# Mirroring a quarter of each symmetric product by VectorE and HBM instead of TensorE, in a four-layer graph network

## The chip, the cores and the metric

The kernel runs on one core of a Trainium2 chip. The metric is device time in microseconds, medians of several runs. A ratio is the mean time of one kernel's runs over that of the other kernel's runs of the same rounds, so it is not quite the ratio of the medians that are quoted.

The engines are TensorE (PE; its weight loads are listed as PEld), VectorE (DVE), ScalarE (ACT), GpSimd (POOL) and SyncE (SP). A name with a q, such as ACTq or SPq, is the sequencer of that engine, which takes instructions in program order and also issues transfers.

## The reference, cut to what matters

There are 16 batches of a graph with 1024 nodes and 128 features, in fp32, and four layers. Two of the layers contain a product whose result is a symmetric matrix. Layer 0 has it three times, layer 3 once (there the kernel multiplies gT by hT in one symmetric product, so that the sum with the transpose needs no pass of its own):

```python
# layer 0, three times
h = h @ W + b
nh = h / jnp.maximum(norm, EPS)
cos = jnp.einsum('bij,bkj->bik', nh, nh)      # symmetric, 1024 x 1024
h = jnp.einsum('bpq,bqc->bpc', edge_weight * cos, h)
# layer 3
h = jnp.einsum('bnf,of->bno', x, W_w) + W_b
e = jnp.einsum('bil,bkl->bik', h @ A, h)
e = e + jnp.swapaxes(e, 1, 2)                 # symmetric, 1024 x 1024
att = jax.nn.softmax(jnp.where(adj > 0, e, 0), axis=1) * adj
...
```

Layer 1 multiplies by the adjacency; layer 2 is an attention with tanh and exp. They matter here only as work beside the products.

## The kernel before

Each symmetric product is 8 x 8 blocks of 128 x 128. The kernel multiplies only the blocks on and above the diagonal. It keeps those above the diagonal in SBUF (the tile `above`, copied out of PSUM by ScalarE) and fills the blocks below by transposing the kept ones on TensorE:

```python
def row_of_square(k, j, s, leftT, rightT, above):      # row j of blocks, half s of it
    lo, hi = HALVES[s]
    dst = ps(f"sq_{k}_{j}_{s}")                         # a PSUM bank
    first = max(lo, j)
    if first < hi:
        pe((hi - first) * MM, ..., lambda: nc.tensor.matmul(dst..., cols(leftT.t, j), span(rightT.t, first, hi)))
    n = min(hi, j) - lo
    if n > 0:
        ...                                             # at: the places of the kept blocks
        def mirrored():
            for r, p in enumerate(at):
                nc.tensor.transpose(cols(dst.t, r), cols(above.t, p), ident)
        pe(n * TR, ...)
    return dst
```

The instructions are not written in the order in which they run. Each is recorded as an `Op` with its engine, an assumed duration and what it reads and writes. A planner then orders all of them, up to three batches interleaved, with constants: a period, latencies, and a table `LEADS` with a number for each kind of instruction. What it decides is fixed; every engine then works through its list in order. A transfer is recorded on an engine "DMA" that holds nobody else.

```python
op("DMA", 2.0, [z], [],
   lambda: nc.scalar.dma_start(out[b]..., by_block(z.t)))   # the store of a batch's result
```

## Time and profile before

| | before |
|---|---|
| median of 4 runs | 2550.4 us |
| TensorE busy | 2500 us, 98% |
| VectorE busy | 2004 us, 79% |
| ScalarE busy | 1385 us, 54% |
| DMA queue of SyncE | 143 MB, 30% of 16 engines |
| period of a batch in the middle | 155.3 us |

The period is read from the chain of work that ended last: the same piece, 22 matmuls of 9.44 us, stands there at 882.60 and at 1037.86 us. An engine's row that says how much it was busy does not yet say what it costs: pipelined matmuls overlap, so work on TensorE is priced by the distance between starts. The prediction does that, and shows the lines.

### The profile page before, as it was taken

Reading aid. Unit: us, or ns where it says so; the run is one execution under the profiler, and the core shown is the slowest. Engines: PE = TensorE matmul, PEld = TensorE weight load, DVE = VectorE, ACT = ScalarE, POOL = GpSimd, SP = SyncE. Lnnn points to the kernel's source line nnn. Section 1 sums busy time; section 2 is a strip of 40 time slices with the busy share of each in tenths; the row PEclk is TensorE's granted clock in tenths of the full one; section 3 lists DMA queues with packets and bytes.
Section 4 is the critical chain, followed back from the end, with each engine's and each line's share of the span. In section 5 each row is a group of like instructions: output and inputs, shape, how many; then the busy total and the mean of one; then the engine's idle time right before and its main releaser. Section 6 shows DMA issues by size and latency. Waiting matters only on the chain.

```text
span 2548.1 us, 35510 instructions
## 1 busy us (share of the span) xinstructions
PE 2500.2 (98%) x12714; PEld 1674.1 (66%) x12714; DVE 2003.7 (79%) x5070; ACT 1384.7 (54%) x2609; POOL 215.3 (8%) x134
## 2 busy tenths in 40 slices
PE   7999999999999999999999999999999999999996
PEld 4567576775667666676666767657676666765763
DVE  6658979787787968879687796877878778796777
ACT  4426575644646556455654656447464564554365
POOL 1001000101101010010100101010010100100000
PEclk9999999999999999999999999999999999999998
DMA  9320706133070430604216052340614306042100
GB/s 138 68 67 4 146 1 101 49 52 98 1 124 26 59 91 11 133 7 67 83 26 123 1 84 66 46 104 1 116 34 59 91 8 122 21 59 75 30 12 17
DMA packets 588641, 154.32 MB, mean 61 GB/s; under 512 B 537520, under 2 KB 572080, under 8 KB 588464
## 3 DMA queue, kind: packets, MB, share of 16 engines
q1 hardware_dynamic: 567552, 142.65, 29.6%
q10 hardware_dynamic: 20912, 9.40, 1.4%
q8 instruction: 100, 1.64, 0.3%
q14 instruction: 77, 0.63, 0.1%
HBM read 143.61 MB, written 8.39 MB: 60 GB/s over the span
## 4 chain that ended last, share of the span: by engine, by line
PE 91%; DVE 4%; ACT 2%; DMA 1%; SPq 1%; issue 1%; POOLq 0%; POOL 0%; ACTq 0%; DVEq 0%
PE acc L620 33%; PE acc L631 18%; PE sq L587 17%; PE sq L597 7%; PE psP L453 5%; PE py L463 2%; PE py L792 2%; PE ps_hTn L443 1%; PE ph L463 1%; PE ps_hnT L443 1%; PE pg L463 1%; PE psN L453 1%; SPq L673 1%; DVE e L921 1%; DVE top L930 1%; ACT e L934 1%
## 5 line engine op out<-in xcount | busy, mean ns | idle before, releaser
L740 DVE SCALAR_TENSOR_TENSOR ew<-sq,rn,adjT 128x512 f32<-128x512 f32 x768 | 555.0, 741 | 133.9 <-PE sq L597 84.4
L609 ACT COPY above<-sq 128x512 f32<-128x512 f32 (+3 forms) x640 | 285.2, 455 | 491.6 <-DVE ew L740 431.1
L620 PE MATMUL acc<-ew,h 128*128 128x512 f32 x1024 | 498.4, 597 | 1.6 <-DVE ew L740 1.5
L587 PE MATMUL sq<-hTn 128*128 128x512 f32 (+3 forms) x1152 | 452.2, 489 | 2.4 <-ACT hTn L475 2.4
L597 PEld LDWEIGHTS sq<-ident,above 128*128 128x128 f32 x1792 | 226.5, 141 | 156.9 <-issue 108.3
L597 PE MATMUL sq<-ident,above 128*128 128x128 f32 x1792 | 299.8, 273 | 4.9 <-ACT above L609 4.9
L620 PEld LDWEIGHTS acc<-ew,h 128*128 128x128 f32 x1024 | 177.2, 191 | 147.0 <-issue 100.2
L587 PEld LDWEIGHTS sq<-hTn 128*128 128x128 f32 x1152 | 189.3, 191 | 121.2 <-issue 84.6
L631 PEld LDWEIGHTS acc<-h,ew 128*128 128x128 f32 x2048 | 244.1, 192 | 31.7 <-issue 14.4
L631 PEld LDWEIGHTS acc<-h,e 128*128 128x128 f32 x2048 | 239.9, 193 | 30.3 <-issue 27.1
L631 PE MATMUL acc<-h,ew 128*128 128x128 f32 x2048 | 251.5, 275 | 0.3 <-DVE ew L740 0.3
L631 PE MATMUL acc<-h,e 128*128 128x129 f32 x2048 | 241.1, 276 | 2.5 <-DVE e L862 2.5
L934 ACT ACTIVATE e<-e,top 128x1024 f32<-128x1024 f32 x128 | 146.9, 1148 | 171.9 <-DVE top L930 166.5
L620 PE MATMUL acc<-e,hs 128*128 128x512 f32 x512 | 235.7, 596 | 1.5 <-DVE e L941 1.5
L620 PE MATMUL acc<-adjL,hn 128*128 128x512 f32 x512 | 236.8, 593 | 0.3 <-ACT hn L567 0.2
L862 DVE SCALAR_TENSOR_TENSOR e<-adjT,e 128x512 f32<-128x512 f32 x256 | 165.2, 686 | 64.0 <-ACT e L858 63.8
L436 POOL TENSOR_TENSOR rstd<-ve,mhalf 128x8 f32<-128x8 f32 x64 | 104.8, 1637 | 1096.0 <-DVE ve L528 1092.6
L684 ACT ACTIVATE adjT<-adjT 128x1024 f32<-128x1024 f32 x128 | 135.3, 1057 | 95.5 <-DVE adjT L681 78.5
L921 DVE SCALAR_TENSOR_TENSOR e<-adjT,sq 128x512 f32<-128x512 f32 x256 | 170.5, 675 | 6.5 <-PE sq L587 6.5
L941 DVE TENSOR_TENSOR e<-e,adjT 128x512 f32<-128x512 f32 x256 | 167.3, 679 | 0.0
L681 DVE STREAM_TRANSPOSE adjT<-adjT 128x1024 f32<-128x1024 f32 x128 | 155.8, 1229 | 8.8 <-DMA adjT<-in_adj_dram 4.6
L620 PEld LDWEIGHTS acc<-adjL,hn 128*128 128x128 f32 x512 | 93.8, 190 | 101.4 <-issue 88.6
(121 smaller groups left out, 3260.8 us busy)
## 6 DMA issues: line engine op xcount, KB each, us to landing
adjT<-in_adj_dram SPq DMA_DIRECT2D x512, 128.0 KB, 3.9
adjL<-in_adj_dram SPq DMA_DIRECT2D x128, 512.0 KB, 4.0
x<-in_x_dram SPq DMA_DIRECT2D x16, 512.0 KB, 5.1
out_dram<-z ACTq DMA_DIRECT2D x16, 512.0 KB, 5.6
b<-in_L_gnn_b_dram ACTq DMA_DIRECT2D x4, 64.0 KB, 4.5
w<-in_L_gnn_W_dram ACTq DMA_DIRECT2D x2, 128.0 KB, 3.9
w<-in_L_gnn_W_dram ACTq DMA_DIRECT2D x3, 64.0 KB, 3.5
w2e<-in_L_gnn_W_dram ACTq DMA_DIRECT2D x1, 64.0 KB, 2.7
```

What stands on the lines that cost most here:

```text
L453: nc.tensor.matmul(dst.t[:, (c - lo) * n : (c - lo + 1) * n], cols(srcT.t, c), w, start=True, stop=True)
L587: lambda: nc.tensor.matmul(dst.t[:, (first - lo) * P :], cols(leftT.t, j), span(rightT.t, first, hi), start=True, stop=True),
L597: nc.tensor.transpose(cols(dst.t, r), cols(above.t, p), ident)
L609: lambda: nc.scalar.copy(span(above.t, p, p + hi - first), dst.t[:, (first - lo) * P :]),
L620: lambda s=s, lo=lo, hi=hi: nc.tensor.matmul(acc[s].t, cols(h.t, at, w), span(ew.t, lo, hi), start=(j == 0), stop=(j == NB - 1)),
L631: nc.tensor.matmul(a.t[:, (c - lo) * n : (c - lo + 1) * n], cols(ew.t, c), h.t[:, j * w : j * w + n], start=(j == 0 and c == lo), stop=(j ...
L681: dve(V(N), [t], [t], lambda t=t: nc.vector.transpose(t.t, t.t), True)
L740: lambda pc=pc, ew=ew, rn=rn, j=j, lo=lo, hi=hi: nc.vector.scalar_tensor_tensor(span(ew.t, lo, hi), pc.t, rn.t[:, j : j + 1], span(aT[j].t ...
L862: lambda e=e, j=j, lo=lo, hi=hi: nc.vector.scalar_tensor_tensor(span(e.t, lo, hi), span(aT[j].t, lo, hi), 0.0, span(e.t, lo, hi), op0=ALU. ...
L921: lambda e=e, p=p, j=j, lo=lo, hi=hi: nc.vector.scalar_tensor_tensor(span(e.t, lo, hi), span(aT[j].t, lo, hi), 0.0, p.t, op0=ALU.is_gt, op ...
L934: lambda e=e, top=top, tot=tot: nc.scalar.activation(e.t[:, 0:N], e.t[:, 0:N], AF.Exp, bias=top.t, accum_out=tot.t),
L941: lambda e=e, j=j, lo=lo, hi=hi: nc.vector.tensor_mul(span(e.t, lo, hi), span(e.t, lo, hi), span(aT[j].t, lo, hi)),
```

## The change

The lower left quarter of each product (rows 4 to 7, columns 0 to 3) is the mirror of the upper right one. The change takes its 16 transposes from TensorE. VectorE turns each 32 x 32 square of the upper right quarter while it reads it out of PSUM. In each product two stores to HBM and eight reads, ten transfers, then put the squares in their places in a tile `got`. The masking passes read `got` from SBUF. This is done in batches 1 to 13. In layer 3, h^T is now a transpose of h rather than a second product. And the buffers and the planner's constants are new.

```diff
+    FAR = range(1, B - 2)
...
+            if self.by_dma and j >= QUARTER and s == 0:
+                q = j - QUARTER
+                return self.got, lambda: self.got.t.rearrange("p (r c d) -> p c r d", r=QUARTER, d=P)[:, q]
...
+            if self.by_dma and j < QUARTER and s == 1:
+                p, above = PLACE[j, lo], self.above
+                dve(
+                    V(HALF), [read], [blk(above, p, p + 4)],
+                    lambda: nc.vector.transpose(span(above.t, p, p + 4), read.t),
+                )
+                if j % 2:
+                    self.send(j - 1, j + 1)
+                return
...
+        def send(self, lo, hi):
+            ...                                  # store of two rows of four blocks, 512 KB
+            op("DMA", 0.35 * (hi - lo), [blk(above, at, end)], [by_hbm], ..., lat=2.2)
+            def squares_to_places():
+                src = by_hbm.t.rearrange("(x j) (g i) -> g j x i", j=SQ, i=SQ)
+                for g in range(P // SQ):
+                    dst = span(got.t, lo * 4, hi * 4)[g * SQ : (g + 1) * SQ]
+                    ...
+                    nc.sync.dma_start(dst.rearrange("p (x i) -> p x i", i=SQ), src[g])
+            op("DMA", 1.8 * (hi - lo), [by_hbm], [blk(got, lo * 4, hi * 4)], squares_to_places, lat=2.4)
...
-        hT, gT = w4(f"h3T_{b}"), w4(f"gT_{b}")
-            for dst, w, v, name in ((hT, w3e[:, 0:D], wb3col, "ph"), (gT, wg, bg, "pg")):
...
+        hT = flipped(h, f"h3T_{b}", w=E3)
...
-    PERIOD, LAST, AHEAD, WINDOW = 74.0, 9.0, 2, 0.02
+    PERIOD, LAST, AHEAD, WINDOW = 66.0, 23.0, 2, 0.05
...                                              # POOLS, KINDS and all of LEADS replaced
```

## The prediction

> **What bounds the kernel now.** I read the page of the profiled execution first, its busy table and the chain of work that ended last:
>
> ```profile
> PE 2500.2 (98%) x12714; PEld 1674.1 (66%) x12714; DVE 2003.7 (79%) x5070; ACT 1384.7 (54%) x2609; POOL 215.3 (8%) x134
> PE 91%; DVE 4%; ACT 2%; DMA 1%; SPq 1%; issue 1%; POOLq 0%; POOL 0%; ACTq 0%; DVEq 0%
> ```
>
> TensorE is busy 98% of the span and carries 91% of the last chain; VectorE is the next, at 79%. Busy time of pipelined matmuls can mislead, so I asked for the busy time by stretch. Two runs of 22 back-to-back L620 matmuls lie 155.2 us apart again and again in the chain, so that is the period of one of the 16 batches. One period, then the first 100 us and the last 99 us (engines PE, PEld, DVE, ACT, POOL, then clock, DMA share, GB/s):
>
> ```profile
> 1041.00:1196.20 155.20, 155.03 (x795) 104.21 (x794) 124.77 (x317) 86.17 (x163) 13.35 (x8) 1.00 0.31 62
> ...
> 0.00:100.00 100.00, 80.92 (x327) 48.05 (x328) 70.45 (x170) 47.95 (x95) 12.20 (x13) 0.97 0.91 131
> ...
> 2450.00:2549.00 99.00, 73.99 (x356) 48.34 (x355) 80.97 (x187) 61.44 (x110) 6.40 (x3) 0.91 0.04 11
> ```
>
> In the middle TensorE lacks 0.17 us of work in a period, VectorE has 30 us free, the DMA engines are busy 31%. About 19 us are lost at the start and 25 at the end. A microsecond taken from TensorE in the middle is therefore a microsecond off the span, as long as VectorE and the transfers keep up.
>
> To price TensorE's work I need the distance between instructions, not their mean duration, which holds the pipeline's depth. The order in time and the chain give it:
>
> ```profile
> 1008.35 1.04 PE L597 MATMUL sq<-ident,above 128*128 128x128 f32 x8
> ...
> 1037.86 9.44 PE acc L620 x22
> ```
>
> Eight transposes take 1.04 us, one alone lasts 0.273 us, so the next starts (1.04 - 0.273)/7 = 0.110 us later. A 512-wide matmul instruction takes 9.44/22 = 0.429 us; a program's 512-wide fp32 product is two of these, 0.858 us. Sixteen 128-wide instructions in 1.95 us give 0.112 us each in the same way. Priced so, all of TensorE's work sums to about 2477 us, which agrees with the busy time.
>
> **What the Trainium skill says.** "Perfetto Trace Analysis", section "Identifying the Most-Contended Engine", says that matmul occupancy does not tell the distance from roofline. This trace agrees that occupancy isn't peak rate (weight loads are busy 66%), but the bound is real: the chain runs through TensorE and its gaps are 0.1%. The gain has to come from fewer instructions.
>
> "VectorE: DVE Perf Modes", section "The three transpose paths", says VectorE's transpose turns 32x32 blocks only, and warns against a plain copy whose strides do the transposing. That is why the change needs a second leg: the blocks are turned on VectorE, and the way through HBM moves whole 32-element rows of squares to their places. The kernel before does the same for the adjacency, and its trace shows both legs: the square transpose of 128x1024 takes 1229 ns, and the transfers are priced below.
>
> "DMA: Bandwidth & Descriptors", sections "Specifications" and "Anatomy of one DMA", says that runs below 512 B miss line rate, and that the fixed cost, some 2 us, is mostly the receipt of the last byte, heaviest into HBM. The trace agrees: a 128 KB transfer in 128-byte runs lands after 2.2 us at best, 3.9 in the median; 512 KB to HBM in 512-byte runs (the store of the output, the very shape of the new store) after 3.2 us at best, 5.6 in the median.
>
> **The change, part by part.** It acts in 13 of the 16 batches (1 to 13), in 4 products each, so 52 squares.
>
> *Removed from TensorE.* In a square, rows 4 to 7 no longer mirror their left half: 4 x 4 = 16 of the 28 transposes go. 16 x 52 = 832 of 1792, and 832 x 0.110 = 91.5 us. The rows they come from and where they go:
>
> ```profile
> L597 PE MATMUL sq<-ident,above 128*128 128x128 f32 x1792 | 299.8, 273 | 4.9 <-ACT above L609 4.9
> L463 PE MATMUL ph<-hnT,w3e 128*128 128x512 f32 x64 | 30.3, 594 | 0.2 <-ACT hnT L475 0.2
> L941 DVE TENSOR_TENSOR e<-e,adjT 128x512 f32<-128x512 f32 x256 | 167.3, 679 | 0.0
> ```
>
> The second row is layer 3's separate projection for h^T: 64 instructions x 0.429 = 27.5 us. It becomes 8 transposes in a batch, 128 x 0.110 = 14.1 us. Saved: 13.4 us, in all 16 batches. TensorE loses 91.5 + 13.4 = 105 us in all: 7.0 + 0.8 = 7.9 us in a period, from 155.2 to 147.3.
>
> *Added to VectorE.* Four transposes of 128x512 from PSUM in each square, 208 in all. I take the occupied time of another pass of that size, 167.3/256 = 0.65 us (third row above): 136 us, 10.5 us in a period. The masking passes that now read the returned blocks from SBUF instead of PSUM keep their count and, as passes with both inputs in SBUF take 679 to 686 ns and those with one in PSUM 675, their price. VectorE goes from 124.8 to 135.3 us of a 147.3 us period, 92%, and from 2004 to 2140 us in all. It stays below TensorE, but its free time shrinks from 30 to 12 us a period.
>
> *Removed from ScalarE.* The 208 512-wide copies of those half rows, about 0.5 us each: 100 us. It is at 54% and off the path, so this is worth nothing by itself.
>
> *Added to the transfers.* In each square two stores of 512 KB and eight reads of 128 KB in 128-byte runs, 4 + 4 MB in a period beside the adjacency. Rates, from two stretches of the kernel before, the first with adjacency squares, the second with 4 KB rows:
>
> ```profile
> 1012.00:1017.00 5.00, 5.00 (x29) 3.41 (x28) 5.00 (x9) 2.34 (x5) 0.00 (x0) 1.00 0.73 108
> ...
> 1067.00:1072.00 5.00, 5.00 (x19) 2.74 (x18) 0.85 (x3) 0.60 (x2) 1.90 (x1) 1.00 0.73 231
> ```
>
> 108/0.73 = 148 GB/s for the small runs when the engines are full, about 316 for the large. 4.2 MB of small runs take 28 us, 4.2 MB of stores some 13 to 20 us. The DMA share goes from 48 us of 155 to about 92 of 147, 60 to 65%: not a bound in the mean.
>
> *The latency of one mirroring.* Store 3.2 to 5.6 us; four reads, 512 KB at 148 GB/s = 3.5 us, plus a landing tail of about 2 us: 9 to 11 us from the last transpose to the data. In the built order of VectorE's instructions, what stands between the last transpose of a square and its first use of the returned blocks is, in one product of layer 0, twelve 512-wide passes (12 x 0.65), eight statistics (8 x 0.21), eight aggregations (8 x 0.08) and a small one: 10.3 us. By the same counting two further products of a period have about 10 us and layer 3's about 20. So the latency is just hidden where the DMA engines are free, and short by a few microseconds where adjacency loads stand in the way.
>
> *The new plan order and buffers.* The built order is again periodic from batch 3 on, with TensorE's priced work in a period at 146.8 us. At both ends it is like the old one: about 40 us of TensorE work stand behind the last layer-3 projection, formerly and now. I book nothing for the ends.
>
> **Sum.** 2551.7 - 105 = 2447 us if TensorE stays as full as it is. I add 13 us: about 1 us a period of TensorE waiting, because VectorE at 92% with transfer waits of a few microseconds in its in-order stream cannot follow as loosely as at 80%. That gives 2460 us, 3.6% faster. The 1 us is my choice; nothing of before measures it.
>
> **Rivals.** *The way through HBM is late.* If each of the three tight products of a period waits 5 us, VectorE has 135 + 15 = 150 us, above TensorE's 147: period about 151, some 50 us of the gain lost, 2500 us. For it: the store of that shape took 5.4 to 5.9 us in the middle of the run, and the queue issues in order, so a read waiting for its store holds up loads behind it. Against: VectorE has 12 us of slack and the reads' rate fits.
>
> *VectorE becomes the local bound.* In the stretch of the old kernel from 1012 to 1042 us it was busy 5.00 of every 5 us, and TensorE still had work queued. Ten more microseconds of it, most in such stretches, and PSUM banks that now wait for two VectorE readers, could cost 2 to 4 us a period: 2475 to 2500 us. Against: during layer 1 VectorE was idle over 80% for ten microseconds, so a new order has something to fill.
>
> *The saving lies beside something else.* If transposes hid in the weight loads or in waits, removing them would give little, and the time would stay near 2540. Against: their spacing, 0.110 us, is in the priced sum that fits the span, and no gaps remain for them to hide in.
>
> *The new order is better at the ends.* 44 us are lost there; 10 us regained makes 2440.
>
> **Range and chances.** Most of what can go wrong costs 15 to 50 us, and only the ends can bring more than 105. 80% range: 2436 to 2502. Faster by over 2% means below 2500.7, that is, losing less than half of the saving: 0.87. Within 2%: 0.10. Slower by over 2% would need transfer waits of some 12 us a period beyond the saving: 0.03.
>
> **What will show it.** Right: TensorE's mirrored transposes at 960 with a period near 148 us and TensorE above 99% in it; 208 VectorE transposes near 0.68 us; VectorE near 87% of the span; waits of VectorE for the returned blocks under 100 us in all, and hardly any of them reaching TensorE. Wrong: TensorE idle for VectorE's products by several microseconds a period (the second rival), or those preceded by VectorE waiting for a transfer (the first), or a period below 147.

## The result, and the profile after

The changed kernel takes 2484.18 us (2483.74 to 2484.56, 4 runs) against 2550.43 us (2548.58 to 2552.96, 4 runs). The ratio is 0.974, with a 95% interval of 0.9723 to 0.9756. It is faster by 2.6%. The time is inside the predicted range, but of the 105 us that were to be saved, 66 arrived.

The busy table and the chain that ended last, of the changed kernel:

```profile
PE 2410.6 (97%) x11946; PEld 1588.7 (64%) x11946; DVE 2119.4 (85%) x5278; ACT 1287.1 (52%) x2401; POOL 214.4 (9%) x134
PE 78%; DVE 9%; ACT 7%; issue 2%; DMA 1%; SPq 1%; ACTq 0%; POOL 0%; POOLq 0%; DVEq 0%
```

TensorE carries 78% of the chain instead of 91%. The rest has gone to VectorE and ScalarE, so TensorE now waits for something. One period, and the two ends (engines in the order PE, PEld, DVE, ACT, POOL, then clock, DMA share, GB/s):

```profile
868.44:1018.40 149.96, 148.17 (x736) 97.54 (x735) 133.53 (x333) 78.79 (x147) 13.09 (x8) 1.00 0.58 119
...
0.00:100.00 100.00, 77.42 (x300) 44.69 (x301) 70.07 (x165) 45.04 (x89) 12.20 (x13) 0.95 0.89 158
2383.00:2482.00 99.00, 74.75 (x358) 48.63 (x356) 82.59 (x191) 61.46 (x109) 5.43 (x3) 0.88 0.04 11
```

The period is 150.0 us; the prediction's price of TensorE's work made 147.3. TensorE is idle 1.8 us of it; the other 0.9 us are counted as busy. The ends lose as much as before, within 4 us. So what is missing is missing in the middle, 13 times 2.7 us or about 35.

The parts of the change, in the table of groups and in the table of issues (for a transfer, the last number is the median time to landing in us):

```profile
L619 PE MATMUL sq<-ident,above 128*128 128x128 f32 x960 | 174.4, 275 | 27.8 <-ACT above L641 27.8
L631 DVE STREAM_TRANSPOSE above<-sq 128x512 f32<-128x512 f32 x208 | 147.0, 707 | 10.5 <-PE sq L609 9.1
L791 DVE SCALAR_TENSOR_TENSOR ew<-got,rn,adjT 128x512 f32<-128x512 f32 x156 | 112.8, 743 | 1.8
...
by_hbm<-above SPq DMA_DIRECT2D x104, 512.0 KB, 3.2
got<-by_hbm SPq DMA_DIRECT2D x416, 128.0 KB, 3.0
```

The counts are as predicted, 960 and 208. A transpose of VectorE takes 707 ns where near 680 was forecast; its start-to-start distance from the next pass is 0.62 us (in the chain below). The passes that read `got` stood idle 1.8 us in all, and no transfer is named for it; the 52 passes of layer 3 that read it (L973) stood idle 0.0 us. So VectorE never waits for the returned blocks. What grew is the first row's wait: TensorE stood idle 27.8 us for `above`, ScalarE's copy, where it was 4.9.

Where that comes from is shown by the chain in order of time (start, length, what) in the same period:

```profile
927.75 1.52 PE sq L609 x4
...
930.70 0.62 DVE above L631
931.32 2.07 DVE z L505 x8
...
936.33 0.96 ACT e L910
937.29 2.60 issue
939.90 0.38 ACTq L1056
...
949.43 0.02 issue
949.45 0.06 DVE e L914
...
954.39 2.09 DVE ew L791 x3
956.48 0.02 issue
956.50 0.49 ACT above L641
956.99 0.04 issue
957.03 0.33 PE sq L619
```

From the end back: TensorE at 957.03 waited for ScalarE's copy of a row of layer 0. That copy waited for VectorE's masking pass of the same row. VectorE came late to it because it had been following ScalarE through the tanh/exp tiles of layer 2 (L914 after L910), one by one. And ScalarE was late with those because between 937.29 and 939.90 it did nothing, and then issued L1056. L1056 is the store of the previous batch's result. ScalarE's own line of time around it:

```profile
936.24 1.06 ACT L910 ACTIVATE e<-e 128x1024 f32<-128x1024 f32 x1
939.90 0.38 ACTq L1056 DMA_DIRECT2D out_dram<-z  x1
940.32 2.19 ACT L906 ACTIVATE e<-s,h 128x1024 f32<-128x1024 f32 x2 [3.03 <-issue]
```

ScalarE idles 3.03 us before a tanh (L906) whose inputs had long been there. The profile calls it "issue" because the tanh itself waits for nothing; it is the store before it in the queue that waits for z, which VectorE finishes at 939.8. How long the store's wait stood in ScalarE's queue, in ns as minimum, median and maximum, for the kernel before and the changed one:

```profile
L1002 ACTq EVENT_SEMAPHORE  x16: 17/982/3401, 305.2 to 2540.4; - x16
```

```profile
L1056 ACTq EVENT_SEMAPHORE  x15: 17/4820/4825, 334.9 to 2474.1; - x15
```

The median went from 1.0 to 4.8 us. The wait is in the kernel before as well, but there, in the period that I looked at, the next thing in ScalarE's queue was a pass of layer 1 that waited for TensorE anyway. In the list of waits (us in total, times, longest) the changed kernel has

```profile
ACT e L906 <- issue: 36.6, 13, 3.1
```

or 2.8 us each, about one in every period; the kernel before has no such entry.

This is theory A: the new order puts the store in front of urgent ScalarE work, because the planner thinks that a store holds nobody. Theory B: VectorE, at 89% of a period, is simply too full, and the store is only where it shows. Theory C: the transfers are late or in the way. Theory D: the new plan order costs something by itself.

### The profile page after: what moved, and what is told of

The parts are those of the page before. It is cut to its first block, busy times and chain, and to the rows that moved or that the text cites. A ratio compares the mean times of both kernels' runs of the same rounds, so it can differ in the third digit from the quotient of the medians. Undisturbed runs are those within 1.5% of the kernel's fastest.

```text
span 2481.8 us, 34726 instructions
## 1 busy us (share of the span) xinstructions
PE 2410.6 (97%) x11946; PEld 1588.7 (64%) x11946; DVE 2119.4 (85%) x5278; ACT 1287.1 (52%) x2401; POOL 214.4 (9%) x134
## 4 chain that ended last, share of the span: by engine, by line
PE 78%; DVE 9%; ACT 7%; issue 2%; DMA 1%; SPq 1%; ACTq 0%; POOL 0%; POOLq 0%; DVEq 0%
PE acc L671 31%; PE sq L609 17%; PE acc L682 11%; PE psP L461 6%; PE sq L619 4%; ACT e L906 3%; DVE ew L791 3%; ACT e L910 3%; PE py L844 2%; PE py L471 2%; DVE e L914 2%; PE ps_hTn L451 1%; DVE z L505 1%; PE pg L471 1%; PE ps_hnT L451 1%
## 5 line engine op out<-in xcount | busy, mean ns | idle before, releaser
L791 DVE SCALAR_TENSOR_TENSOR ew<-sq,rn,adjT 128x512 f32<-128x512 f32 x612 | 436.9, 739 | 68.2 <-PE sq L619 32.0
L671 PE MATMUL acc<-ew,h 128*128 128x512 f32 x1024 | 480.6, 597 | 4.7 <-DVE ew L791 4.5
L609 PE MATMUL sq<-hTn 128*128 128x512 f32 (+3 forms) x1152 | 441.3, 489 | 0.4 <-ACT hTn L483 0.4
L641 ACT COPY above<-sq 128x384 f32<-128x384 f32 (+3 forms) x432 | 169.2, 394 | 403.9 <-DVE ew L791 366.5
L682 PE MATMUL acc<-h,e 128*128 128x129 f32 x2048 | 249.5, 277 | 2.8 <-DVE e L914 1.5
L619 PEld LDWEIGHTS sq<-ident,above 128*128 128x128 f32 x960 | 125.7, 141 | 142.2 <-issue 74.0
L619 PE MATMUL sq<-ident,above 128*128 128x128 f32 x960 | 174.4, 275 | 27.8 <-ACT above L641 27.8
L914 DVE SCALAR_TENSOR_TENSOR e<-adjT,e 128x512 f32<-128x512 f32 x256 | 162.0, 683 | 41.9 <-ACT e L910 41.9
L732 DVE STREAM_TRANSPOSE adjT<-adjT 128x1024 f32<-128x1024 f32 x128 | 155.2, 1225 | 17.8 <-DMA adjT<-in_adj_dram 10.9
L906 ACT ACTIVATE e<-s,h 128x1024 f32<-128x1024 f32 x128 | 143.1, 1141 | 38.4 <-issue 36.6
L631 DVE STREAM_TRANSPOSE above<-sq 128x512 f32<-128x512 f32 x208 | 147.0, 707 | 10.5 <-PE sq L609 9.1
```

The costliest lines, as they stand in the source:

```text
L609: lambda: nc.tensor.matmul(dst.t[:, (first - lo) * P :], cols(leftT.t, j), span(rightT.t, first, hi), start=True, stop=True),
L641: lambda: nc.scalar.copy(span(above.t, p, p + hi - first), read.t[:, (first - lo) * P :]),
L671: lambda s=s, lo=lo, hi=hi: nc.tensor.matmul(acc[s].t, cols(h.t, at, w), span(ew.t, lo, hi), start=(j == 0), stop=(j == NB - 1)),
L682: nc.tensor.matmul(a.t[:, (c - lo) * n : (c - lo + 1) * n], cols(ew.t, c), h.t[:, j * w : j * w + n], start=(j == 0 and c == lo), stop=(j ...
L732: dve(V(N), [t], [t], lambda t=t: nc.vector.transpose(t.t, t.t), True)
L791: lambda view=view, ew=ew, rn=rn, j=j, lo=lo, hi=hi: nc.vector.scalar_tensor_tensor(by_block(span(ew.t, lo, hi), D, 4), view(), rn.t[:, j ...
```

## The experiments

### The store on SyncE's queue

```diff
-            lambda: nc.scalar.dma_start(out[b]..., by_block(z.t)),
+            lambda: nc.sync.dma_start(out[b]..., by_block(z.t)),
```

> The changed kernel with one word altered: the store of the output is issued from SyncE's queue instead of ScalarE's. Every instruction of TensorE, VectorE and GpSimd stands in the same order. Theory A (ScalarE stands behind its own store: its queue waits 4.8 us in the median for z, then the tanh/exp pairs of layer 2 start 2.8 us late, VectorE follows them, and TensorE waits some 2 us for a copy of layer 0): the period falls from 150.0 to about 148 us, TensorE's waits for the copy above (27.8 us) go to under 5, the time to about 2458 us, 1.0% below the changed kernel. Theory B (VectorE at 89% of the period is what TensorE waits for) and theory C (the transfers, which share SyncE's queue, are late): no change at 2484, or with C a few us slower.

Measured: 2453.79 us (2453.39 to 2454.57, 4 runs; before 2551.11), ratio 0.9617, interval 0.9604 to 0.963. That is 30.4 us below the changed kernel, 4 us more than theory A asked for. One forecast of theory A was missed: TensorE's wait for ScalarE's copy fell from 27.8 us, but to 9.0 and not under 5. That wait, one period, and ScalarE's line of time at the same place:

```profile
PE sq L619 <- ACT above L641: 9.0, 5, 2.3
```

```profile
788.72:936.07 147.35, 147.35 (x737) 97.54 (x736) 133.70 (x333) 78.55 (x148) 13.35 (x8) 1.00 0.60 122
```

```profile
929.50 1.06 ACT L910 ACTIVATE e<-e 128x1024 f32<-128x1024 f32 x1
930.46 2.18 ACT L906 ACTIVATE e<-s,h 128x1024 f32<-128x1024 f32 x2
```

The tanh pair now follows the exp with no gap. TensorE is busy 147.35 us of 147.35, and the period is the one that the prediction priced. Since TensorE, VectorE and GpSimd have the very same lists here, theory A holds for 30 of the missing 35 us, and B, C and D don't explain those 30. This version beats both kernels.

### The same word in the kernel before

The edit is the same, in the kernel before.

> Control: the kernel before with the same word altered. There ScalarE's queue waits only 1.0 us in the median at the store and TensorE never waits in the middle, so theory A expects 2550 us as before, within 3 us. If moving the store helps every kernel (a cheaper queue, say), this one would gain 20 us too, and theory A falls.

Measured: 2551.60 us (13 runs) against 2551.11, ratio 1.000, interval 0.9992 to 1.0009. The queue by itself is worth nothing. It is the wait in front of urgent work that costs.

### The plan told of the hold

```diff
-        op(
-            "DMA", 2.0, [z], [],
+        o = op(
+            "ACT", 0.4, [z], [],
             lambda: nc.scalar.dma_start(out[b]..., by_block(z.t)),
         )
+        o.key = "3 DMA z"
```

> The changed kernel with the store still in ScalarE's queue, but the plan told so: it is booked as a ScalarE instruction that waits for z, not as a transfer that holds nobody. The order of all engines changes with it. Theory A (the plan did not know that the store holds ScalarE): the plan keeps other ScalarE work ahead of the store, the hold per batch falls from 2.8 us to under 1, and the time is within 12 us of the 2454 of the kernel with the store on SyncE. If it is the ScalarE queue as such that is slow at stores, it stays near 2484.

Measured: 2621.58 us (4 runs), ratio 1.0284, so worse than both theories said. Theory A's forecast, within 12 us of 2454, was not met. The hold did become rarer: "ACT e L906 <- issue" is down to 18.5 us in 6 occurrences, though the store's wait is still 3.4 us in the median. But the whole order changed with it, and in the new order TensorE is busy only 289 of 300 us in the middle. So the run neither supports nor refutes theory A: what the changed order cost and what the rarer hold gained can't be told apart. It does show that this planner's order can go bad when one cost is altered under a table of leads that was made for another.

### No mirroring, new plan

```diff
-    FAR = range(1, B - 2)
+    FAR = ()
```

> The changed kernel with no batch mirrored by VectorE and HBM: only layer 3's h^T turned from h, and the new plan constants, remain. TensorE's priced work falls by 13.4 us against before, to 2463. If the plan itself is sound: 2538 us, 0.5% faster than before. The plan's constants were sought for the other set of instructions, so theory D (the new plan order costs something by itself) expects 2550 or more.

Measured: 2580.78 us (4 runs), ratio 1.0115, interval 1.0101 to 1.0129. Theory D is right for this set of instructions: with 13 us less work for TensorE than the kernel before, it is 30 us slower. Here the store's wait is 17 ns in the median, so it isn't the store. The period is 156.35 us. The plan's constants are not better or worse as such; they fit the set with mirroring.

### The old constants with mirroring

```diff
-    PERIOD, LAST, AHEAD, WINDOW = 66.0, 23.0, 2, 0.05
+    PERIOD, LAST, AHEAD, WINDOW = 74.0, 9.0, 2, 0.02
     LEADS = {
-        ...                      # all values of the changed kernel
+        ...                      # all values of the kernel before
```

with the store on SyncE.

> Store on SyncE, mirroring and buffers as in the changed kernel, but the plan's constants (PERIOD, LAST, WINDOW, LEADS) of the kernel before. The instructions are the same, in another order. If the order must be sought for the very set of instructions, as the run without mirroring suggests (30 us slower than before in the new order): 2490 to 2600. If any order of this planner would do: about 2455.

Measured: 2712.43 us (4 runs), ratio 1.0627: outside my range, 259 us worse than the same instructions in the new order. TensorE carries only 56% of its chain. So the new order is no ornament of the change: in the old order, mirroring by VectorE would have lost. The old table has no entries for the new instructions, which then count as 0; how much of the 259 us that makes, I did not test.

### All batches mirrored

```diff
-    FAR = range(1, B - 2)
+    FAR = range(B)
```

with the store on SyncE.

> Store on SyncE and all 16 batches mirrored by VectorE and HBM instead of 13: TensorE's priced work falls by another 3 x 7.0 = 21 us, which would make 2433 if the ends can follow and the order in the middle stays as good. But the plan's order changes everywhere, and VectorE has under 1 us of slack a period: I expect 2440 to 2520, so rather a loss than a gain.

Measured: 2729.21 us (4 runs), ratio 1.0693, again far outside my range. The extra mirroring is worth 21 us of TensorE at most; the order, which changed everywhere with it, cost more than ten times that. In the middle, where the instructions are the same, TensorE is busy 280 of 300 us. Whether mirroring at the ends is good or bad can't be read from this run.

### TensorE's remaining transposes twice

```diff
                         nc.tensor.transpose(cols(dst.t, r), cols(above.t, p), ident)
+                        nc.tensor.transpose(cols(dst.t, r), cols(above.t, p), ident)
```

with the store on SyncE.

> Store on SyncE, same order, and each of TensorE's remaining 960 mirrored transposes done twice. If a transpose of TensorE costs its spacing, one for one, as the prediction priced it: 960 x 0.110 = 105 us more, 2559 us (VectorE then has slack again, so nothing else is added). If transposes partly lie beside other work, it is clearly less, say under 2520.

Measured: 2544.87 us (2542.81 to 2546.31, 7 runs), ratio 0.9974, interval 0.9964 to 0.9985. It costs 91 us, between the two forecasts (105 us, or under 66), and so is far from hidden. In the middle the period goes from 147.35 to 152.17 us, 4.8 for 48 transposes priced at 0.110, or 5.3. The missing 0.5 us are short delays that the busy table does not show and that are gone with the doubled work: before doubling, three runs of matmuls of the period took longer in the chain than the same matmuls elsewhere (16 in 2.02 us instead of 1.79, 12 in 5.29 instead of 5.15, 6 in 2.64 instead of 2.58), 0.43 us in all, and with doubling none does. In the run itself the doubled transposes follow each other at 0.11 us. The rest of the difference to 105 us must lie outside the middle, where TensorE waits anyway; I did not follow it. So the price that the prediction put on a transpose is right where TensorE is full.

### VectorE's transposes twice

```diff
-                    lambda: nc.vector.transpose(span(above.t, p, p + 4), read.t),
+                    twice,      # the same transpose, two times
```

(The edit is shortened: `twice` calls the transpose two times.) First with the store on ScalarE as in the changed kernel:

> The changed kernel with each of the 208 square transposes of VectorE done twice, in the same order: VectorE gains 208 x 0.62 = 129 us of work, 9.9 us a period, which makes 133.6 + 9.9 = 143.5 us of a 150.0 us period. Theory B: VectorE's load is what costs, so nearly all of it comes out: the period grows by 5 to 10 us, the time to 2550 to 2610. Theory A: VectorE has slack except behind the late tanh/exp pairs, and the period grows by under 4 us, to under 2535.

Measured: 2588.42 us (4 runs), ratio 1.0144; 104 us more than the changed kernel, of 129 us of added work. This is what theory B forecast, and theory A's forecast (under 2535) failed: VectorE has no 9.9 us a period to spare. Then with the store on SyncE:

> Store on SyncE, all 208 square transposes done twice: 129 us more VectorE work, 9.9 us a period, VectorE at 143.9 of 147.3 us if nothing waits. With the store on ScalarE the same doubling cost 104 us. If the 104 us were VectorE's order alone, it costs 95 to 110 us here too (2550 to 2565); if part of it was the two waits meeting (the hold of ScalarE grew from 2.8 to 3.9 us in that run), it costs 60 to 90 us (2514 to 2544).

Measured: 2564.20 us (2558.73 to 2569.84, 4 runs), ratio 1.0053; 110 us more than without doubling. So the cost is there without the hold of ScalarE, and that the hold grew in the other run added nothing. Then with only row 0's transpose doubled, 52 of 208:

> Store on SyncE, and one of the four square transposes of each square (row 0's) done twice: 52 x 0.62 = 32 us more VectorE work, 2.5 us a period, VectorE at 134.0 + 2.5 = 136.5 of 147.3 us. If VectorE has slack now (TensorE's gaps are nil in the middle): under 5 us more, below 2459. If it is the bound beside TensorE (theory B): about 30 us more, 2484.

Measured: 2474.26 us (2472.69 to 2476.19, 4 runs), ratio 0.970; 20.5 us more for 32 us of work. Neither forecast was met; the truth lies between. The three runs together: the first 32 us of added work cost 20.5, the next 97 cost 90. VectorE shows 13.6 us of idle time in a period of 147.35 us, yet of 2.5 us put in, only about 1 disappeared in it: the same piece of the chain stands at 1538.35 and 1687.30 us, a period of 148.95 us. The trace of the version without doubling shows where the idle time lies. In ten-microsecond stretches of one period VectorE is busy 9.99 and 10.00 us from 976 to 996 us, where transposes of its squares stand, and only 5.43 from 1036 to 1046. Part of the cost may also come by another way, as a later transpose makes its transfers later: in the run with row 0 doubled the chain of one period holds the landing of a read, 2.85 us. I did not separate the two. Theory B is therefore not the cause of the 30 us that came back with the store moved, but VectorE has about 1 us a period left before it costs.

### The reads twice

```diff
                         nc.sync.dma_start(dst.rearrange("p (x i) -> p x i", i=SQ), src[g])
+                        nc.sync.dma_start(dst.rearrange("p (x i) -> p x i", i=SQ), src[g])
```

with the store on SyncE.

> Store on SyncE, and every read of the mirrored blocks back from HBM done twice (16 reads of 128 KB in a square instead of 8): the DMA engines' share rises from 59% to about 80% of the middle, and each square's data comes some 4 us later, as the second read of a place must be waited for too. If the transfers have that much slack, the time stays within 5 us of 2454; theory C (they arrive just in time) expects 3 waits of 3 to 4 us a period in VectorE and 30 to 100 us more.

Measured: 3402.43 us (4 runs), ratio 1.3339. This was a badly made experiment: the second read writes where the first one writes, so SyncE waits for the first to land before it issues the second, as the list of SyncE's waits says (total us, times, longest):

```profile
SPq L663 <- DMA got<-by_hbm: 958.5, 416, 5.0
```

416 waits of 2.3 us turn the reads, which otherwise run beside each other, into a row. It measures that and not the load. So I mended it, with the second reads going to a tile of their own:

```diff
+                        spare = span(scratch, 0, (hi - lo) * 4)[g * SQ : (g + 1) * SQ]
+                        nc.sync.dma_start(spare.rearrange("p (x i) -> p x i", i=SQ), src[g])
```

> Store on SyncE, same order, and behind each read of mirrored blocks a second read of the same data into a tile that nobody uses, so that no read waits for its twin (that wait spoilt the earlier doubling of the reads). SyncE issues 8 more transfers in a square at some 0.6 us each and the DMA share goes to about 80%; the last wanted read is issued some 2 us later. If the transfers have slack: within 10 us of 2454. If they arrive just in time (theory C): 3 late squares a period at 2 us or more, which with VectorE at its limit comes out in full: 2500 to 2530.

Measured: 2718.80 us (4 runs), ratio 1.0653; 265 us more, beyond theory C's range. The first use of returned blocks in a square, in VectorE's line of time and in the list of waits:

```profile
1045.65 1.41 DVE L794 SCALAR_TENSOR_TENSOR ew<-got,rn,adjT 128x512 f32<-128x512 f32 x2 [3.55 <-DMA got<-by_hbm]
...
DVE ew L794 <- DMA got<-by_hbm: 111.2, 31, 6.0
DVE e L976 <- DMA got<-by_hbm: 57.1, 12, 5.8
```

Now VectorE does wait for the transfers, 168 us in 43 waits. Two things can have delayed the last wanted read, and the run does not separate them. Eight more transfers of a square are issued in SyncE's queue, at 0.56 us and more each. And although the DMA share is 63% over the span, an average misleads here: from 1030 to 1045 us, where the reads for the first line above stand, it is 1.03 (the view's figure can pass 1), and from 1080 to 1165 us 0.98, so the engines are about full when the squares move; without the spare reads it is 0.92 from 985 to 1050 us. The wanted reads land after 3.8 us in the median instead of 3.1. The slack of the good version can be read from its own trace. In one period the last read of a layer-0 square is issued at about 940.3 us and lands about 2.9 us later, at 943.2; VectorE uses it at 944.65. Followed in the same way, with the median landing of their group of reads, two other squares of the period had about 1.5 and 2 us. So the transfers of the version with the store on SyncE are on time by one to two microseconds, as estimated from one period and from landings that are partly medians. Theory C is not the cause of the missing time, but there is little room before it would cost; the forecast that the transfers have slack (within 10 us of 2454) failed. Why 168 us of direct waits become 265 us of time I did not follow further; waits for adjacency loads also grew, to 52.0 us from 15.5.

## Why the prediction was right or wrong

**What bounds the kernel, and the removed work: right.** The step "105 us in all: 7.0 + 0.8 = 7.9 us in a period, from 155.2 to 147.3" is confirmed by the run with the store on SyncE: 147.35 us, TensorE busy all of it by the table, 2453.8 us against the 2447 of the sum. (The period of the kernel before is 155.26 us by the chain; the prediction read 155.2.) The doubled transposes confirm the price from the other side. The rival that the saving lies beside something else is refuted.

**VectorE: right in size, too comfortable in words.** It was priced at 2140 us in all and 135.3 us a period; it measured 2119 and 133.5 to 133.7. "Its free time shrinks from 30 to 12 us a period" is right as idle time (13.6 in the good version), but it is not slack: the doubling of a few transposes found about 1 us. The rival "VectorE becomes the local bound" did not take the missing time, since moving the store gave 30 us back with VectorE's work unchanged; but its reason, stretches in which VectorE has no gap, is what the doubled transposes ran into.

**The latency of one mirroring: right, and a bit better.** I had 9 to 11 us from last transpose to data; in one period of the version with the store on SyncE it was from 935.04 to 943.2, 8.2 us. The store to HBM landed after 3.2 us in the median, near the best of the old store rather than its median. The rival "the way through HBM is late" did not come: no wait of VectorE for returned blocks to speak of. That it would have been dear is shown by the run with spare reads.

**The step that was mis-sized: "I add 13 us: about 1 us a period of TensorE waiting, because VectorE ... with transfer waits of a few microseconds in its in-order stream cannot follow as loosely".** The term measured 37 us, or 2.7 us a period, of which 30 are one thing, and it is none that I named: the store of the output in ScalarE's in-order queue, whose wait for z held up the tanh/exp tiles of layer 2. ScalarE I had dismissed with "at 54% and off the path". The mark of this was in the built order, and in the trace of before: ScalarE's store had a wait of 1.0 us in the median, and the new order put layer 2's tanh behind it. I looked only at what stood between VectorE's instructions. Of the remaining 7 us about 5 lie at the ends: in the version with the store on SyncE TensorE is idle 25.7 us of the first 100 and 23.8 of the last 99, where it was 19.1 and 25.0 before. What holds it there is not shown.

That the time still fell into the range is partly luck. The range left room for waits of VectorE and of the transfers; the room was used up by a wait of ScalarE.

**The signs.** 960 and 208 came as said, VectorE's share (85% for 87%) nearly, and VectorE waited for no returned block. The main sign failed: the period is 150.0 us and not near 148, and TensorE is at 98.8% of it and not above 99%. TensorE's idle time followed ScalarE's copies, which none of the signs of being wrong named. One phrase of the chances is wrong as written: 2% slower, or 2603 us, needs 12 us a period in all (156 us in 13 periods), of which about 4 are beyond the saving.

**The new plan order: nearly right to book nothing at the ends (3 to 5 us more are lost there), wrong not to say what hung on it.** I treated it as neutral. The runs show that for a given set of instructions the order is worth hundreds of microseconds: 259 between the two tables of constants. "The new order is better at the ends" did not come.

The Trainium skill could have warned me: "DMA: Bandwidth & Descriptors", section "Anatomy of one DMA", says that any wait of a transfer for a semaphore happens on the issuing sequencer before dispatch. Followed to its end, a store issued from an engine that also computes can hold that engine's next instruction. This trace agrees, with 3.03 us.

## What to carry to other kernels

Ask of every transfer from whose queue it is issued, what it waits for there, and what stands behind it; an engine at 52% can hold the one that bounds the kernel, and a planner that books transfers as holding nobody can put one in front of urgent work. Idle time marked "issue" in front of an instruction whose inputs were ready came, in this case, from the instruction before it in that queue. When two engines are both near full and their orders are fixed, an idle share is not slack: measure it by adding a little work, look in which stretches the idle time lies, and don't expect a fixed table of priorities to survive a change of the work: in four runs here it did not.

## What the Trainium skill lacked or had wrong

- "DMA: Bandwidth & Descriptors", section "Issuing engines are not separate DMA queues", says that issuing from several engines only saves the time of initiating on the sequencer. This section lacks the other side, which follows from the sentence of the same page that is quoted above: an engine that issues a transfer which is not ready can stand still. Moving one store a batch from ScalarE to SyncE took 30.4 us of 2484 off, and nothing off the kernel in which the work behind it wasn't urgent.
- The same page's fixed cost is fitted to the path from GpSimd, which the prediction did not say when it used it; of what the cost consists, no run here shows. For transfers issued from SyncE these runs show, from issue to landing in the middle of a busy kernel: 512 KB to HBM in 512-byte runs 2.9 to 4.8 us, median 3.2; 128 KB from HBM in 128-byte runs 2.1 to 5.3 us, median 3.0; and 0.56 us of SyncE's queue in the median for each of the latter.
- "VectorE: DVE Perf Modes", section "The three transpose paths", gives times for bf16 alone. In fp32, VectorE's square transpose of 128x512 out of PSUM took 707 ns (0.62 us until the next pass could start), and TensorE's transposes of 128x128 followed each other at 0.110 us, one alone lasting 0.273 us.
- No page that I read says how much of the idle time of an engine can take added work: VectorE was idle 13.6 us of 147.35, and 2.5 us of added work lengthened the period by 1.6 us.
